# Another order at the seams of a six-stage kernel: expert stages, recurrence gates, layernorms in quarters, first rotations on another engine

## The chip, the cores and the metric

The kernel runs on one core of a Trainium2 chip. The metric is the device time of one execution in microseconds (us). A core has five engines that matter here, each of which works through its own instructions in order: PE (TensorE, the matmuls), DVE (VectorE), ACT (ScalarE), POOL (GpSimd) and SP (SyncE, which issues most of the transfers). They wait for each other through semaphores.

## The reference

The input x has 2 sequences of 2048 tokens with 256 features, 4096 tokens in all. Six residual stages follow each other:

```python
x = x + 0.5 * moe(layernorm(x))       # stage 1
x = x + attention0(layernorm(x))      # stage 2
x = x + 0.5 * moe(layernorm(x))       # stage 3, the same weights
x = x + 0.5 * rnn(layernorm(x))       # stage 4
x = x + attention1(layernorm(x))      # stage 5
x = x + 0.5 * rnn(layernorm(x))       # stage 6

# moe: sigmoid router, 2 of 6 experts, and one shared expert
w, idx = top_k(sigmoid(xt @ gate_w.T + gate_b), 2);  w = w / (sum(w) + 1e-8)
y = sum over the chosen e of w_e * ((silu(xt @ ew1[e].T) * (xt @ ew3[e].T)) @ ew2[e].T)
z = (silu(xt @ fc1.T) * (xt @ fc2.T)) @ fc3.T
moe = y + z

# attention0: 16 heads of 16 features over the full sequence of 2048, then Wff and a bias
# attention1: the same shape, causal, with rotated q and k, and relative
#             positions clipped at 32 in both the scores and the context

# rnn: the first axis (2) is the time; 2048 columns are the batch
c = in_c
for xt in x:                          # 2 steps
    f = sigmoid(xt @ wf.T + c @ uf.T + bf);  i = sigmoid(xt @ wi.T + c @ ui.T + bi)
    c = f * c + i * tanh(xt @ wc.T + c @ uc.T + bc)
rnn = tanh(x @ wo.T + c @ uo.T + bo)
```

All is computed in 32-bit floats.

## The kernel before

x stays in the on-chip memory for the whole run, as 32 chunks of 128 tokens by 256 features. Four chunks make a block (512 tokens), so there are 8 blocks; blocks 0 to 3 are the first sequence, 4 to 7 the second. The order on PE, ACT and DVE is the order in which the program issues its instructions; inside the expert stage the same holds for POOL. Nothing reorders the work afterwards, so an instruction that waits holds everything behind it on its engine. Results of matmuls go to 8 banks of 512 floats (`s` in the profile), which ACT or DVE must empty before PE can use them again.

**Layernorm** (lines 86 to 124). `stat(b, c)` runs two DVE instructions on one chunk (L95, L96), `root(b)` two on POOL for the block (L100, L102), `stats(b)` is four `stat` and the `root`. `normal(b, engine)` applies mean and scale with four instructions (L113) on DVE or POOL, `turn(b)` transposes the block on PE (L123) and copies it out on ACT (L124).

**Expert stage, `moe`** (L158 on). The router (`route`, L184) computes logits on PE (L190), copies them with ACT (L195), transposes them (L198), and picks two experts on DVE. `sort` (L237) gives each token a place per expert, `scatter(b)` (L298) writes the normalized rows of one block to those places in DRAM: 8 indirect transfers on POOL's queue. `experts(h, ...)` (L332 to L395) then works through the sorted rows of one half of the tokens, which SP loads (`xs<-places`). `combine(h, c)` (L398 to L410) fetches the two weighted results of one chunk, again with an indirect transfer on POOL (`yg`, L403), and adds them to x on DVE (L408). The shared expert is cut into `shared_up` (16 matmuls, L138, and Silu on ACT, L311), `shared_mul` (DVE, L318) and `shared_down` (16 matmuls L325, added to x by DVE, L330). An explicit list at L420 to L473 interleaves all of this: blocks 0 to 3 are normalized, routed, sorted and scattered, then 4 to 7; `experts(0)`, `experts(1)` with the chunks of the first half combined in between; at the end the shared expert of blocks 5, 6 and 7 and 16 chunks of `combine(1, c)`, 8 in a row, then block 7, then 8 more.

**Recurrence** (L730 on). `gate(cb, step, m)` makes three matmul groups for one block at one time step, activations on ACT (L781), products on DVE (L786 on). `outputs(cb)` computes both steps' outputs (L802 and L816 on PE, L821 and L827 on DVE, L824 on ACT). After `outputs(cb - 1)` a call `between(cb - 1)` runs; in the first recurrence it contains the layernorm and turn of blocks 0 and 1 for the second attention, and some preparation of its weights.

**Attentions** (L609 and L861 on). Both run through a table of steps: `jobs.at(step, fn, ...)` registers work beside the score matmuls, and the work of one step is issued in the order in which it was registered, half of it after the first and half after the second piece of the step. Score matmuls for the row maximum (L650, L969) feed DVE reductions (`mx`, L654 and L977); `subtract(t)` transposes the negative maxima of a group (L545) and adds them to q on DVE (L549), after which the scores for the exponential can be computed (L662, L1047 and L1054). `ln_stats(b, qc)` runs the statistics of one block in one step, its `normal` on POOL. In the second attention `rotate` (L890) copies a projection out of PSUM (ACT, L896), exchanges neighbours (DVE, L898) and does the multiplications and the addition on POOL (L899 to L903).

Of the kernel before, what the change touches and what calls it, by code (L numbers as in the profile page):

```python
# [17 lines left out]
P = 128  # L18
# [24 lines left out]
def macaron_kernel(ctx: ExitStack, tc: tile.TileContext, t: dict, out: bass.AP):  # L43
# [114 lines left out]
    def moe(w, ws, gate_w, gate_b, rev, tri, iota, z, behind, last):  # L158


        with ExitStack() as s:
# [9 lines left out]
            def norm(b):  # L171
                if b not in xn:
                    z.normal(b, nc.vector, keep.tile([P, CPB, D], F32, name=f"xn{b}"))
                if b not in xnT:
                    z.turn(b)

            def stats(b):
                if b not in xn:
                    z.stats(b)
# [4 lines left out]
            def route(h):  # L184
# [27 lines left out]
                col = [keep.tile([P, HC, 1], F32, name=f"col{h}{i}") for i in range(4)]  # L212
# [24 lines left out]
            def sort(h):  # L237
# [41 lines left out]
                at = place[h] = keep.tile([P, 2 * HC], mybir.dt.int32, name=f"at{h}")  # L279
# [24 lines left out]

            def shared_up(b):
                pgu = [bank() for _ in range(4)]
                for i in range(4):
                    mm2(pgu[i], ws[:, :, i // 2 * D : i // 2 * D + D], ts(i % 2, P), xnT[b])
                sgs = [wk.tile([P, TB], F32, name="sgs", bufs=4) for _ in range(2)]
                for ic in range(2):  # L310
                    nc.scalar.activation(sgs[ic], pgu[ic], AF.Silu)  # L311
                half[b] = sgs, pgu[2:]

            def shared_mul(b):
                sgs, pu = half.pop(b)
                hh[b] = wk.tile([P, 2, TB], F32, name="hh", bufs=2)
                for ic in range(2):
                    nc.vector.tensor_tensor(hh[b][:, ic, :], sgs[ic], pu[ic], ALU.mult)  # L318
# [79 lines left out]
            def combine(h, c):  # L398

                for i in range(2):  # L400
                    yg = wk.tile([P, D], F32, name="yg", bufs=6)
# [18 lines left out]
            with tc.manual_schedule(engines={mybir.EngineType.Pool}):  # L420
                for b in range(HB):
                    stats(b)
                    norm(b)
                    if b == 1:
                        up(0)
                route(0)
                mul(0)
                stats(4)
                stats(5)
                up(1)  # L430
                down(0)
                e0 = sort(0)
                scatter(0)
                stats(6)
                stats(7)
                for b in range(1, HB):
                    scatter(b)
                mul(1)
                up(2)
                norm(4)  # L440
                norm(5)
                mul(2)
                down(1)
                up(3)
                norm(6)
                norm(7)
                mul(3)
                down(2)
# [3 lines left out]
                down(3)  # L452
                e1 = sort(1)
                for b in range(HB, NTB):
                    scatter(b)
                down(4)
                experts(0, e0, lambda i: None)
                experts(1, e1, first_half)
                up(5)
                mul(5)  # L460
                up(6)
                mul(6)
                down(5)
                for c in range(8):
                    combine(1, c)
                    last(c)
                up(7)
                mul(7)
                down(6)
                down(7)  # L470
                for c in range(8, HC):
                    combine(1, c)
                    last(c)  # L473
            xnT.clear()

# [9 lines left out]
    class Pieces:  # L485
# [14 lines left out]
        def ln_stats(self, b, qc):  # L500
            blk = b * SB + qc
            self.norm.stats(blk)
            self.norm.normal(blk, nc.gpsimd)
            self.add_bias(blk)
# [104 lines left out]
    def attention0(norm, tail, wq, wk_, wv, wo, bff):  # L609
# [7 lines left out]
        with ExitStack() as s:  # L617
# [64 lines left out]
            PER = 8  # L682
            for b in range(B):
                first = b * SB * G * PER

                for qc in range(SB) if b else ():
                    at(first - 40 + 4 * qc, z.ln_stats, b, qc)
# [4 lines left out]
                for g in range(G):  # L692
                    for qc in range(SB):
                        due = first - 6 + PER * g + qc
                        at(due if b else (-1 if g == 0 else 2 * g - 1 + qc // 2), keys, b, g, qc)
# [4 lines left out]
            for t, (b, qc, g) in enumerate(groups):  # L700
                at(PER * t - 1, queries, t)
                at(PER * t + 8, z.subtract, t)
# [27 lines left out]
    def recurrence(w, norm, store, between):  # L730
# [3 lines left out]
        with ExitStack() as s:  # L734
# [106 lines left out]
            for m in range(2):  # L841
                gate(0, 0, m)
            turn(1)
            for cb in range(SB):
                if cb + 1 < SB:
                    for m in range(2):
                        gate(cb + 1, 0, m)
                if cb + 2 < SB:
                    normal(cb + 2)
                gate(cb, 1, 0)  # L850
                if cb + 2 < SB:
                    turn(cb + 2)
                gate(cb, 1, 1)
                if cb:
                    outputs(cb - 1)
                    between(cb - 1)
# [4 lines left out]
    def attention1(norm, tail, w, relk, relv, kbias, dramp, skew):  # L861
# [4 lines left out]
        with ExitStack() as s:  # L866
# [23 lines left out]
            def rotate(dst, wa, b, qc, bias):  # L890
# [8 lines left out]
                nc.gpsimd.tensor_tensor(dst, xa, cos[b, qc], ALU.mult)  # L899
                nc.gpsimd.tensor_tensor(xb, xb, sin[b, qc], ALU.mult)  # L900
                if bias is not None:
                    nc.gpsimd.tensor_scalar_add(xb, xb, bias)
                nc.gpsimd.tensor_tensor(dst, dst, xb, ALU.add)  # L903
# [240 lines left out]
            for n in range(NG):  # L1144
                at(early[n], queries, n)
            for b in range(B):
                for qc in range(SB):
# [5 lines left out]
                    if b or qc > 1:  # L1153
                        at(f - 12, z.ln_stats, b, qc)
# [6 lines left out]
            for n, (b, qc, g) in enumerate(groups):  # L1161
                at(max(By[n], early[n] + 1), by_position, n)
                at(Me[n] + 1, z.subtract, n)
# [47 lines left out]
    def run_moe(norm, behind, last, clear=False):  # L1211
        with ExitStack() as s:
# [16 lines left out]
            moe(w, ws, gate_w, gate_b, rev, tri, iota, norm, behind, last)  # L1229
# [36 lines left out]
    with tc.manual_schedule(engines=ENGINES):  # L1266

        n0, n1, n2, n3, n4, n5 = (Norm() for _ in range(6))
        with ExitStack() as s:
# [10 lines left out]
            for b in range(3):  # L1280
                tail += [(1 + 2 * b, n2.stats, b), (2 + 2 * b, n2.normal, b, nc.vector),
                         (3 + 2 * b, n2.turn, b)]
            attention0(n1, tail, *weights)
# [3 lines left out]
        with ExitStack() as s:  # L1287
# [13 lines left out]
            run_moe(n2, ahead.run, last)  # L1301
# [7 lines left out]
            def between(cb):  # L1309

                if cb == 0:
# [6 lines left out]
                if cb in (1, 2):  # L1318
                    n4.stats(cb - 1)
                    n4.normal(cb - 1, nc.vector)  # L1320
# [98 lines left out]
```

## Time and profile before

| | |
|---|---|
| median of 3 runs | 4281.56 us (4280.34 to 4281.79) |
| the profiled execution, its own time | 4388.43 us |
| its span | 4386.7 us |
| mean granted PE clock | 0.971 |
| PE busy | 4143.3 us |
| DVE, ACT, POOL busy | 2714.8, 2545.9, 1824.1 us |

The stages in this span, by the first instruction of each: first expert stage from 0, first attention from about 430, second expert stage from 2193, recurrence from 2613, second attention from 2816, second recurrence from about 4200 us.

In a row such as "PE s L123 <- DVE b L113: 16.8, 8, 8.0", PE waited before its instruction of line 123 for the DVE instruction of line 113, 16.8 us in all, 8 times, 8.0 us at most. In a timeline row the first two numbers are start and duration, and the square bracket tells how long the engine had been idle and what ended that. In a row of windows the numbers are the window, its length, the busy time of PE, of PE's weight loads, of DVE, ACT and POOL (with the number of instructions), the granted PE clock, the DMA share and the GB/s. The profiled execution is 106.9 us longer than the median of the runs.

### The profile page before, as it was taken

How to read it: one execution, taken by the hardware profiler on the slowest of the kernel's cores; microseconds unless marked ns; L12 is line 12 of the kernel's file. 1: busy time of each engine (PE TensorE's matmuls, PEld its weight loads, DVE VectorE, ACT ScalarE, POOL GpSimd, SP SyncE). 2: the span in 40 equal slices, each digit the busy share in tenths (PEclk: the TensorE clock that was granted, in tenths of full speed). 3: DMA queues.
4: the chain of work that ended last, by engine and by line, in shares of the span. 5: the costliest groups of instructions: out<-in, count | busy, mean ns of one | idle time of the engine just before them, and what ended most of it. 6: DMA issues, size and time to landing. Idle time of an engine off the chain costs nothing.

```text
span 4386.7 us, 77337 instructions
## 1 busy us (share of the span) xinstructions
PE 4143.3 (94%) x28512; PEld 1982.5 (45%) x28512; DVE 2714.8 (62%) x6176; ACT 2545.9 (58%) x5155; POOL 1824.1 (42%) x1665
## 2 busy tenths in 40 slices
PE   6798999999999999999977989799999999999999
PEld 3455433333334333333344554455554455555445
DVE  4233787877776778788551333466676666666633
ACT  2232488887877788888822313155656665566742
POOL 3226133335433333333432240375655774654510
PEclk8899999999999999999988989999999999999999
DMA  6242000000000000000043320144542234542201
GB/s 237 93 121 75 1 1 1 1 1 1 1 1 2 1 1 1 1 1 1 16 148 99 120 82 0 37 94 87 109 88 51 59 76 87 100 95 46 44 21 39
DMA packets 355514, 224.29 MB, mean 51 GB/s; under 512 B 146625, under 2 KB 338497, under 8 KB 355137
## 3 DMA queue, kind: packets, MB, share of 16 engines
q1 hardware_dynamic: 342848, 185.77, 17.2%
q0 software_dynamic: 12288, 33.57, 2.4%
q8 instruction: 227, 3.72, 0.4%
q14 instruction: 151, 1.23, 0.1%
HBM read 114.17 MB, written 105.12 MB: 50 GB/s over the span
## 4 chain that ended last, share of the span: by engine, by line
PE 85%; DVE 5%; POOL 4%; issue 3%; another core or an unknown queue 1%; ACT 1%; DMA 1%; SPq 0%; POOLq 0%; ACTq 0%; DVEq 0%
PE s L662 13%; PE s L674 11%; PE s L138 11%; PE s L650 10%; PE s L1083 6%; PE s L358 6%; PE s L969 6%; PE s L1054 5%; PE s L377 3%; PE s L592 1%; PE s L1064 1%; PE s L527 1%; PE s L1047 1%; PE s L1068 1%
## 5 line engine op out<-in xcount | busy, mean ns | idle before, releaser
L560 POOL TENSOR_TENSOR o<-o,part 128x512 f32<-128x512 f32 (+3 forms) x800 | 964.5, 1206 | 1382.1 <-ACT part L558 1378.2
L654 DVE TENSOR_REDUCE mx<-s 128x1 f32<-128x512 f32 x2048 | 1271.1, 683 | 363.7 <-PE s L650 363.4
L667 ACT ACTIVATE pT<-s 128x512 f32<-128x512 f32 x2048 | 1064.3, 617 | 205.1 <-PE s L650 203.9
L650 PE MATMUL s<-kT,q 32*128 32x512 f32 x4096 | 1014.5, 618 | 7.3 <-DVE mx L654 6.0
L662 PE MATMUL s<-q,kT 32*128 32x512 f32 x4096 | 1014.9, 615 | 6.3 <-DVE q L549 5.4
L1075 ACT ACTIVATE pT<-s 128x512 f32<-128x512 f32 (+3 forms) x1280 | 589.0, 541 | 243.4 <-PE s L1054 105.7
L662 PEld LDWEIGHTS s<-q,kT 32*128 32x128 f32 x4096 | 414.5, 184 | 471.4 <-DVE mx L654 310.5
L558 ACT COPY part<-s 128x512 f32<-128x512 f32 (+3 forms) x800 | 466.1, 584 | 240.2 <-PE s L1083 118.5
L977 DVE TENSOR_REDUCE mx<-s 128x1 f32<-128x512 f32 (+1 forms) x768 | 472.8, 678 | 188.7 <-PE s L969 180.1
L674 PE MATMUL s<-pT,v 128*32 128x512 f32 x4096 | 549.9, 605 | 2.0 <-DVE mx L654 1.9
L650 PEld LDWEIGHTS s<-kT,q 32*128 32x128 f32 x4096 | 405.1, 184 | 138.5 <-ACT pT L667 71.6
L969 PE MATMUL s<-kT,q 32*128 32x512 f32 (+7 forms) x2240 | 333.3, 436 | 4.9 <-ACT part L558 4.6
L358 PE MATMUL s<-we,xT 128*128 x592 | 289.9, 613 | 35.3 <-issue 25.8
L1083 PE MATMUL s<-pT,v 128*32 128x512 f32 (+3 forms) x2560 | 305.5, 545 | 2.3 <-DVE mx L977 1.2
L365 DVE TENSOR_TENSOR h<-sg,s 128x256 f32<-128x256 f32 x148 | 62.1, 421 | 350.0 <-ACT sg L363 299.9
L403 POOL DMA_INDIRECT yg<-results,at x128 | 125.9, 984 | 310.6 <-PE s L358 104.3
L969 PE MATMUL s<-b,q 32*128 32x512 f32 (+7 forms) x1280 | 238.9, 517 | 7.4 <-POOL b L903 4.0
L993 DVE CUSTOM_DVE_ANT_0 band<-s,band 128x160 f32<-128x160 f32 (+1 forms) x512 | 155.7, 316 | 142.4 <-PE s L969 78.3
L1054 PE MATMUL s<-q,kT 32*128 32x512 f32 (+3 forms) x1152 | 240.5, 516 | 0.0
L674 PEld LDWEIGHTS s<-pT,v 128*32 128x32 f32 x4096 | 82.1, 108 | 337.6 <-ACT pT L667 281.9
L1054 PE MATMUL s<-q,b 32*128 32x512 f32 (+3 forms) x896 | 210.7, 568 | 0.0
L1007 POOL TENSOR_TENSOR band<-band,mneg 128x640 f32<-128x640 f32 x128 | 161.3, 1262 | 100.1 <-DVE mneg L1003 99.8
(208 smaller groups left out, 5554.8 us busy)
## 6 DMA issues: line engine op xcount, KB each, us to landing
band<-skew SPq DMA_DIRECT2D x32, 1280.0 KB
pd<-band SPq DMA_DIRECT2D x32, 1280.0 KB
xs<-places SPq DMA_DIRECT2D x148, 128.0 KB
results<-y SPq DMA_DIRECT2D x148, 128.0 KB
places<-zero SPq DMA_DIRECT2D x2, 4736.0 KB
we<-in_we SPq DMA_DIRECT2D x12, 768.0 KB
skew<-s SPq DMA_DIRECT2D x32, 256.0 KB
s<-pd SPq DMA_DIRECT2D x32, 256.0 KB
```

Of the source, the lines that this page charges most:

```text
L138: nc.tensor.matmul(ps, lhsT=w[:, kc, cols], rhs=rhs[:, kc, :], start=start and kc == 0, stop=stop and kc == 1,)
L358: nc.tensor.matmul(pu, lhsT=xT[i][:, ts(kc, P)], rhs=w[:, kc, ds(val[i], 2 * D)], start=kc == 0, stop=kc == 1,)
L560: nc.gpsimd.tensor_tensor(o, o, part[:, q0:], ALU.add)
L650: nc.tensor.matmul(ps, lhsT=q[t][rows(j), ts(qb, P)], rhs=kT[b, g][rows(j), ts(kc, TB)], start=True, stop=True,)
L654: nc.vector.tensor_reduce(mx[t][:, qb * J + j, kc : kc + 1], ps, AX.X, ALU.max)
L662: nc.tensor.matmul(st, lhsT=kT[b, g][rows(j), ts(kb, P)], rhs=q[t][rows(j), :], start=True, stop=True,)
L667: nc.scalar.activation(z.pTs[t, kb, j], st, AF.Exp)
L674: nc.tensor.matmul(pv[rows(j), :], lhsT=v[b, g // 2][:, kb, ds(h * VW, 32)], rhs=z.pTs.pop((t, kb, j)), start=True, stop=True,)
L969: nc.tensor.matmul(ps[:, ds(cols, n)], lhsT=lhsT, rhs=kT[b, c, g][rows(j), ds(k0, n)], start=True, stop=True,)
L1054: nc.tensor.matmul(ps[:, q0:], lhsT=k, rhs=q[t][rows(j), q0:], start=True, stop=True, skip_group_check=True,)
L1075: nc.scalar.activation(z.pTs[t, kb, j][:, q0:], st.pop((t, kb, j))[:, q0:], AF.Exp)
L1083: nc.tensor.matmul(pv[rows(j), q0:], lhsT=v[b, kb // CPB, g // 2][:, kb % CPB, ds(h * VW, 32)], rhs=z.pTs.pop((t, kb, j))[:, q0:], start=T ...
```

## The change

1. The explicit order of the expert stage is rewritten. Statistics of several blocks are issued ahead of the normalizations, the first shared block is computed in four parts between them, `sort(0)` follows the router with only one block's `up` in between, the scatters of blocks 0 to 3 are spread out, and the shared expert's `up`, `mul` and `down` of block 5 come ahead of `experts(0)`. Each Silu directly follows its matmuls (`shared_part`), with 6 buffers instead of 4.
2. At the end, the chunks of `combine(1, c)` are issued in portions (2, 1, 1, 4, then all others) between the shared expert's pieces of blocks 6 and 7. In the second expert stage the last 8 chunks are not issued there but by the recurrence, two after each of its first four gates (`rest`), with 12 buffers for the fetched rows instead of 6.
3. In the first recurrence the layernorms for the second attention are issued ahead of a gate of the second step and their turns behind it (`normals`, `turns`).
4. In both attentions the layernorm statistics are issued one chunk a step, `subtract` is registered ahead of all other work of its step, and in the first attention eight instead of four key projections precede the first step.
5. Rotations of steps before 0 do their multiplications and additions on DVE instead of POOL.

```diff
 def norm(b):
+    normal(b)
+    if b not in xnT:
+        z.turn(b)
+def stats(b):
+    if b not in xn and b not in z.mv:
+        z.stats(b)
+def normal(b):
     if b not in xn:
         z.normal(b, nc.vector, keep.tile([P, CPB, D], F32, name=f"xn{b}"))
...
+def shared_part(b, i):
+    ps = bank()
+    mm2(ps, ws[:, :, i // 2 * D : i // 2 * D + D], ts(i % 2, P), xnT[b])
+    if i < 2:
+        sgs = wk.tile([P, TB], F32, name="sgs", bufs=6)
+        nc.scalar.activation(sgs, ps, AF.Silu)
+        ps = sgs
+    half.setdefault(b, []).append(ps)
...
-                    yg = wk.tile([P, D], F32, name="yg", bufs=6)
+                    yg = (wk if gathered is None else gathered).tile(
+                        [P, D], F32, name="yg", bufs=6 if gathered is None else 12
+                    )
...
-for b in range(HB):
-    stats(b)
-    norm(b)
-    if b == 1:
-        up(0)
-route(0)
+stats(0); stats(1); norm(0); stats(2); norm(1)
+shared_part(0, 0); shared_part(0, 1)
+stats(3); norm(2)
+shared_part(0, 2); norm(3); shared_part(0, 3)
 mul(0)
 stats(4)
+route(0)
+up(1)
+e0 = sort(0)
 stats(5)
-up(1)
 down(0)
-e0 = sort(0)
 scatter(0)
-stats(6)
-stats(7)
-for b in range(1, HB):
-    scatter(b)
 mul(1)
 up(2)
+stats(6); up(3); scatter(1); mul(2)
 norm(4)
 norm(5)
-mul(2)
+stats(7); scatter(2); scatter(3)
 down(1)
-up(3)
+mul(3); down(2)
 norm(6)
 norm(7)
-mul(3)
-down(2)
+down(3)
 route(1)
 up(4)
 mul(4)
-down(3)
 e1 = sort(1)
+down(4); up(5); mul(5)
 for b in range(HB, NTB):
     scatter(b)
-down(4)
+down(5)
 experts(0, e0, lambda i: None)
 experts(1, e1, first_half)
-up(5)
-mul(5)
 up(6)
 mul(6)
-down(5)
-for c in range(8):
-    combine(1, c)
-    last(c)
+rest(2)                  # two chunks of combine(1, c) and last(c)
 up(7)
 mul(7)
+rest(1)
 down(6)
+rest(1)
 down(7)
-for c in range(8, HC):
-    combine(1, c)
-    last(c)
+rest(4)
+if gathered is None:
+    rest(HC)
...
-        def ln_stats(self, b, qc):
+        def ln_stats(self, b, qc, c):
             blk = b * SB + qc
-            self.norm.stats(blk)
-            self.norm.normal(blk, nc.gpsimd)
-            self.add_bias(blk)
+            self.norm.stat(blk, c)
+            if c == CPB - 1:
+                self.norm.root(blk)
+                self.norm.normal(blk, nc.gpsimd)
+                self.add_bias(blk)
...
+            for t in range(NG):
+                at(PER * t + 8, z.subtract, t)
...
-                    at(first - 40 + 4 * qc, z.ln_stats, b, qc)
+                    for c in range(CPB):
+                        at(first - 43 + 4 * qc + c, z.ln_stats, b, qc, c)
...
-                        at(due if b else (-1 if g == 0 else 2 * g - 1 + qc // 2), keys, b, g, qc)
+                        at(due if b else (-1 if g < 2 else 2 * g - 1 + qc // 2), keys, b, g, qc)
...
             for m in range(2):
                 gate(0, 0, m)
+                rest(2)
             turn(1)
             for cb in range(SB):
                 if cb + 1 < SB:
                     for m in range(2):
                         gate(cb + 1, 0, m)
+                        rest(2)
                 if cb + 2 < SB:
                     normal(cb + 2)
+                normals(cb)
                 gate(cb, 1, 0)
                 if cb + 2 < SB:
                     turn(cb + 2)
+                turns(cb)
                 gate(cb, 1, 1)
                 if cb:
                     outputs(cb - 1)
-                    between(cb - 1)
...
-                nc.gpsimd.tensor_tensor(dst, xa, cos[b, qc], ALU.mult)
-                nc.gpsimd.tensor_tensor(xb, xb, sin[b, qc], ALU.mult)
+                e = nc.vector if step < 0 else nc.gpsimd
+                e.tensor_tensor(dst, xa, cos[b, qc], ALU.mult)
+                e.tensor_tensor(xb, xb, sin[b, qc], ALU.mult)
                 if bias is not None:
-                    nc.gpsimd.tensor_scalar_add(xb, xb, bias)
-                nc.gpsimd.tensor_tensor(dst, dst, xb, ALU.add)
+                    e.tensor_scalar_add(xb, xb, bias)
+                e.tensor_tensor(dst, dst, xb, ALU.add)
...
             for n in range(NG):
+                at(Me[n] + 1, z.subtract, n)
+            for n in range(NG):
                 at(early[n], queries, n)
...
-                        at(f - 12, z.ln_stats, b, qc)
+                        for c in range(CPB):
+                            at(f - 13 + c, z.ln_stats, b, qc, c)
                         at(f - 7, z.ln_transpose, b, qc)
...
-            def between(cb):
-                if cb == 0:
-                    ...
-                if cb in (1, 2):
-                    n4.stats(cb - 1)
-                    n4.normal(cb - 1, nc.vector)
-                    n4.turn(cb - 1)
-                    n4.xn.pop(cb - 1)
+            def normals(cb):
+                if cb == 1:
+                    ...                      # the same preparation of a["q"], relk, relv
+                if cb > 1:
+                    n4.stats(cb - 2)
+                    n4.normal(cb - 2, nc.vector)
+            def turns(cb):
+                if cb > 1:
+                    n4.turn(cb - 2)
+                    n4.xn.pop(cb - 2)
```

## Prediction

> **What bounds the kernel now.** I read the page's busy shares and chain first, then the table of windows, then the waits of PE, and last the timeline around the longest of these waits.
>
> ```profile
> span 4386.7 us, 77337 instructions
> PE 4143.3 (94%) x28512; PEld 1982.5 (45%) x28512; DVE 2714.8 (62%) x6176; ACT 2545.9 (58%) x5155; POOL 1824.1 (42%) x1665
> PEclk8899999999999999999988989999999999999999
> PE 85%; DVE 5%; POOL 4%; issue 3%; another core or an unknown queue 1%; ACT 1%; DMA 1%; SPq 0%; POOLq 0%; ACTq 0%; DVEq 0%
> ```
>
> PE bounds the span. The change takes no matmul away, so it can only win PE's idle time, 4386.7 - 4143.3 = 243 us, and what PE loses at a low clock. The clock row dips in two places, the two expert stages.
>
> ```profile
> 410.00:433.00 23.00, 16.84 (x52) 9.57 (x52) 10.77 (x21) 3.35 (x5) 14.51 (x16) 0.78 0.30 86
> 2590.00:2633.00 43.00, 24.39 (x83) 15.71 (x84) 18.85 (x47) 4.37 (x7) 23.57 (x25) 0.72 0.26 74
> 2816.00:2870.00 54.00, 41.05 (x213) 21.22 (x213) 34.29 (x103) 9.63 (x16) 48.65 (x39) 0.87 0.35 83
> 2870.00:4200.00 1330.00, 1292.01 (x11338) 673.83 (x11337) 859.07 (x2562) 837.91 (x1778) 790.21 (x697) 0.99 0.37 78
> ```
>
> [...] The seams are poor (24.4 of 43 us busy at clock 0.72), attention is full. POOL is busy 48.65 of 54 us at the second attention's start.
>
> ```profile
> PE s L198 <- ACT lgT L195: 38.4, 4, 18.9
> PE s L123 <- DVE xn L113: 29.1, 4, 8.9
> PE s L325 <- DVE hh L318: 19.0, 2, 17.8
> PE s L123 <- DVE b L113: 16.8, 8, 8.0
> 98.89 0.59 ACT L195 COPY lgT<-s 128x512 f32<-128x512 f32 x1 [20.68 <-remote]
> 405.37 3.62 PE L325 MATMUL s<-ws,hh 128*128 128x256 f32 x16
> 415.47 6.65 PE L325 MATMUL s<-ws,hh 128*128 128x256 f32 x16 [6.49 <-DVE x L408]
> 423.95 1.07 POOL L403 DMA_INDIRECT yg<-results,at  x1 [3.97 <-DVE x L408]
> 2758.27 0.45 PE L123 MATMUL s<-ident,b 128*128 128x128 f32 x1 [7.13 <-DVE b L113]
> 1016.81 0.66 PE L662 MATMUL s<-q,kT 32*128 32x512 f32 x1 [1.41 <-DVE q L549]
> 2831.32 1.18 PE L969 MATMUL s<-b,q 32*128 32x480 f32 x4 [4.02 <-POOL b L903]
> ```
>
> The longest wait is a doubtful one. The lgT copy needs only a matmul that ended at 80.6, yet runs at 98.9, when the last of 24 scatters in a row has been issued; PE, ACT and DVE all crawl until then. Four such stretches (19 and 20 us in the first expert stage, 18 and 21 in the second), with their half-clock restarts, come to some 100 us. The profiled execution took 4388.4 us, the median of the runs is 4281.6: 107 us less. I therefore take the crawl to belong to the profiled execution, win nothing there, and set the sum of the other stalls against 4281.6.
>
> **The change part by part.**
>
> *Second expert stage into recurrence.* The shared expert's up is 16 matmuls, 7.0 us; its down 3.6 us. Ahead of the gap at 2589.05 PE does up(5), up(6), up(7), down(5), down(6) = 28.3 us, so the experts end at about 2560.7 (the same count gives 381 in the first stage). The first gate matmul comes at 2617.4, 56.7 us later: DVE has 16 gathered rows and two layernorms in front of hh of block 7 (the 17.8 us wait). Afterwards PE has up(6), up(7), down(6), down(7) = 21.2, the bias matmuls L746 2.7, the turn 1.7: 25.6 us. That is 31 us less, 10.6 of which are up(5) and down(5), now in front. The 1.3 us wait for gf goes too. Is DVE in time? The 16 gathers ahead of the recurrence start 3.4 us after the experts (384.7 against 381.3), at a pitch of 1.255 us, and land 2.7 us later: DVE reaches the first bias at +27 us, ACT needs it at about +31. The other 16 gathers (20 us on POOL), 16 adds (0.48 us each) are cut into fours behind the first four gates (12 matmuls, 5.2 us each); four gathers take 5.0 us, so the cover is thin, but they start 3 us ahead. Were the cover gone, they would cost 5 us for each of four. Twelve buffers instead of six let POOL run ahead. **32 us.**
>
> *Front, both stages.* With scatters 0 to 3 out earlier (sort(0)'s 6.3 us DVE chain no longer queues behind two blocks of statistics, 2 x 2.1 us, and a 1.25 us add), the 8.7 us wait at 50.6 goes, with about 3 us of half clock; up(5) and down(5), 10.6 us, come in ahead of experts(0). New: the roots of blocks 6 and 7 stand on POOL behind 8 and 16 scatters of 1.27 us, so norm(7) may hold DVE and PE about 3 us; the 32 scatters of blocks 4 to 7 pass no other work on POOL. SP's loads of xs wait for scatters 0 to 3 as before. The experts start about 2 us later with 10.6 us more done: **-2 us each**, between +5 and -8; the first stage's scatter might also be held by the 4.7 MB fill of places, whose landing I can't see.
>
> *First expert stage into attention.* Here the end is set by POOL: 32 gathers took from 384.7 to 436.35, 51.6 us, though 32 x 1.255 = 40.2; in the rest POOL waited for buffers while DVE stood at mul and down (3.97 us in the row above, 7.9 at 392). With two chunks, mul(7), then single chunks between the downs, the buffers come free in time: 11 us. The clock (6.65 against 3.62 us for the same 16 matmuls): 1.5. Four more keys (7 us of PE) drawn into the wait of 5.95 us at 433.4: 3, since the half-steps they leave fall to what DVE allows, 2.5 instead of 3.0 us. **15 us.**
>
> *Recurrence.* The turns wait 7.13 and 7.96 us for a layernorm behind outputs on DVE (2.1 statistics, 1.5 root, 1.4 normal). They move to a gate of 24 matmuls, 10.6 us. The first is covered; for the second DVE's output tail runs 7 us past PE, and 7 + 5 - 10.6 leaves 1.5. So 13.5. The four a_q/relk operations move under another gate, where they cost nothing; without cover they are 4 x 0.7 = 3 us. The half clock after each gap is a window of 6.8 us, 4.5 us of it busy: 2 us each. **17 us.**
>
> *First rotations on VectorE.* POOL ran 11 operations of 1.27 to 1.57 us from 2816.8 to 2831.3. DVE's tensor_tensor of this shape takes 0.69 (L786); with three shuffles of 0.73 the same takes 9.8 us: b at 2826.7, 4.6 us earlier. Half clock: 1.5. Behind them on DVE's queue stand the first mx reductions, which can't start before b. **6 us**, from 0 to 11. Here a rule speaks against the change. The row: POOL 1.27 us an operation while DVE idles 7.6 us. The Trainium skill, "SBUF — State Buffer", section "SBUF: two separate sides", says that a VectorE operation with two SBUF inputs and a GpSimd operation that reads SBUF exclude each other for the whole instruction. If each of the 11 met a 1.27 us POOL operation, that would be 14 us and the part would lose 8. But the change empties POOL there (its zeroing of v ends at 2815.6), so I keep 6; the row of later rotations decides.
>
> *Layernorm in quarters, subtract first.* In the first attention PE waited 0.93 + 1.41 us twice, because four pairs of statistics (2.1 us) stood ahead of subtract; one pair (0.53) behind it now. 4.7 + 1.5 half clock = 6. In the second: 4.06 us at 2859, half of 5.6 us near 3380 to 3396 (POOL's normal of 4 x 1.22 us stays), and half clock 3: 9. The last quarter comes two steps later, three steps ahead of its turn; a step is about 8.7 us (statistics 2860.5, turn 2903.8, five steps), POOL needs 6.1. **15 us.**
>
> The clock is the second place where row and rule part:
>
> ```profile
> 1069.60:1073.00 3.40, 1.42 (x12) 0.27 (x10) 3.37 (x8) 1.64 (x4) 2.46 (x3) 1.00 0.00 0
> 1073.00:1076.40 3.40, 3.03 (x16) 1.32 (x16) 1.14 (x3) 0.96 (x2) 3.40 (x4) 0.56 0.00 0
> ```
>
> In these 3.4 us PE still worked 1.42 us, and the next 3.4 us ran at 0.56. "TensorE: Matmul & The Clock Gate", Part 1, lets the half clock follow a whole idle window of about 3.4 us; by that, waits of 1 to 3 us cost only themselves, and this part would be worth about 3 us less. The measurement decides, but not each time: the twin waits at 1013.4 and 1015.4 were followed by clock 1.00. So I count one half-clock window here, not two, and my rows of clock stand (about 17 us of the sum in all).
>
> Tiles moved to smaller buffers and the Silu right after its matmul: nothing, ACT is 58% busy and idle there.
>
> Sum: 32 - 4 + 15 + 17 + 6 + 15 = 81 us, 4281.6 - 81 = 4200.
>
> **The rivals.**
>
> (1) *Stalls move.* DVE and POOL run in order. rest(2) makes DVE wait for gathers inside the recurrence, the roots wait behind scatters, mx behind the rotations. For: DVE's waits for yg were 31.8 us in 38. Price: 4 x 5 us in the recurrence, 2 x 8 in front, 6 at the rotations = 42: 4242. Against: POOL is only 10.31 us busy in the recurrence.
>
> (2) *The crawl is real in all runs.* It begins some 11 scatters into a row. The first row, 24 long, is cut to 8, 8, 16: 14 us less in each stage, 28 in all: 4172. Against: the 107 us.
>
> (3) *Slower: subtract waits at PE's head.* Subtract's four transposes are registered first in each of 64 groups; PE is in order, and they need the last mx of the group. If each waited for DVE's last four reductions (2.45 us), that is 157 us, and 4281.6 - 81 + 157 = 4358. It decides from 1.3 us a group (81 / 64). Against: PE's waits for L545 before are 0.4 us in all, and only steps with another job change.
>
> (4) *The diff does less than it says*: the starts stay bound by ws, fill and gathers, the gaps re-form elsewhere: within 0.2%.
>
> **How the numbers follow.** Main case 60%: 4175 to 4225. Rival 1, 22%: 4225 to 4262. Rival 2, 11%: 4150 to 4180. Rival 3, 3%. Rival 4, 4%. 0.2% is 8.6 us, about what a measurement of this kernel can tell from no change. The range 4163 to 4245 leaves out the slow half of rival 1, part of rival 2, and rivals 3 and 4: under 20%. Faster 0.93, same 0.04, slower 0.03.
>
> **What would show it.** Right: L325 <- hh from 19 to under 4 us; L123 <- b under 5; the last yg of the first stage some 44 us after the experts; PE busy over 90% between the experts' end and the second attention; no 8.7 us gap before L123 near 50. The profiled span should fall by about as much as the runs, and more only if the scatters' crawl shrinks. Wrong: waits of PE for L781 or DVE's x L408 inside the recurrence (rival 1), long waits before L545 (rival 3), POOL's rotations slowed by DVE.

## The result and the profile after

The changed kernel takes 4205.97 us (median of 4 runs, 4205.13 to 4206.97), the kernel before 4281.37 us beside it (4280.34 to 4281.79). That is 75.4 us less, a ratio of 0.9824 (95% interval 0.9807 to 0.9841). On two of the chips used, every run of the kernel before takes about 4393 us instead of 4281, and its trace shows all engines late beside the scatters (the crawl, below); the profile shown of before comes from such an execution, those of after from one without it, so the spans of the two must not be subtracted.

The page of the kernel after: span, busy time, granted clock and the chain that ended last.

```profile
span 4204.5 us, 77295 instructions
PE 4101.3 (98%) x28512; PEld 1966.6 (47%) x28512; DVE 2720.4 (65%) x6190; ACT 2542.8 (60%) x5155; POOL 1804.3 (43%) x1651
PEclk9999999999999999999999999999999999999999
PE 90%; DVE 4%; POOL 3%; issue 1%; DMA 1%; ACT 1%; SPq 0%; POOLq 0%; ACTq 0%; DVEq 0%
```

PE is now busy for 98% of the span and both dips of the clock row are gone. What is left shows in the waits of PE (total, times, longest):

```profile
PE s L123 <- DVE xn L113: 25.8, 6, 9.4
PE s L123 <- DVE b L113: 15.5, 7, 12.0
PE s L682 <- DVE mx L686: 8.9, 1, 8.9
PE s L1007 <- DVE b L941: 3.3, 1, 3.3
PE s L202 <- ACT lgT L199: 3.0, 4, 0.8
PE s L335 <- DVE hh L328: 0.4, 2, 0.2
```

(L123 is the layernorm's turn, L202, L335 and L682 are the old L198, L325 and L650, L1007 is the old L969.) The 17.8 us wait for hh fell to 0.4 in all, and the 8.7 us gap near 50 is gone. But the turns did not fall below 5 us as foretold: they wait 12.0 us in the recurrence, behind its first two gates, and 6.4 us in each front (the stretch of an expert stage ahead of its first expert matmul). The windows around the seams, in the columns used before:

```profile
345.00:384.00 39.00, 29.46 (x97) 15.90 (x96) 19.34 (x39) 6.69 (x10) 27.98 (x52) 0.94 0.33 97
2446.00:2497.00 51.00, 38.15 (x130) 22.09 (x130) 19.87 (x51) 6.60 (x11) 30.10 (x32) 0.89 0.36 112
2672.00:2697.00 25.00, 21.06 (x125) 10.67 (x124) 23.55 (x74) 2.93 (x5) 15.60 (x13) 0.93 0.50 126
2697.00:4002.00 1305.00, 1285.86 (x11371) 670.07 (x11372) 870.26 (x2591) 838.21 (x1780) 801.83 (x708) 0.99 0.36 79
```

The two new waits before L123 in the timeline, with what stands ahead of them on POOL and DVE:

```profile
72.10 0.96 POOL L303 DMA_INDIRECT places<-xn,at  x1 [0.30 <-issue]
73.09 0.24 POOL L100 TENSOR_SCALAR ve<-mv 128x4 f32<-128x4 f32 x1
75.06 1.03 PE L123 MATMUL s<-ident,xn 128*128 128x128 f32 x3 [6.42 <-DVE xn L113]
...
2490.11 0.25 POOL L100 TENSOR_SCALAR ve<-mv 128x4 f32<-128x4 f32 x1
2491.59 1.06 POOL L102 TENSOR_TENSOR rstd<-ve,mhalf 128x4 f32<-128x4 f32 x1
2492.68 1.42 DVE L113 TENSOR_SCALAR b<-x,mv,rstd 128x256 f32<-128x256 f32 x4 [9.42 <-POOL rstd L102]
2493.24 1.03 PE L123 MATMUL s<-ident,b 128*128 128x128 f32 x3 [12.00 <-DVE b L113]
```

Both are a root (0.24 + 1.04 us of work) that waits on POOL behind indirect transfers: 8 scatters at 73, and at 2490 a row of 17 gathers, of which the last 9 are for chunks that nobody needs yet. DVE had the statistics ready at 2483.2, so about 8 of the 12.0 us are the root's (6.9 us until it starts, 1.2 for a gather between its two instructions).

For the accounting every trace is divided at the starts of the same instructions: the first expert matmul (L368), the last one (L387), the 65th score matmul of the first attention (L682) and its last (L694), the first and last expert matmul of the second stage, the first gate matmul, the first rotated product (L970), the 41st score matmul behind it that reads a kT and the last score matmul (L1092). Lengths in us; the last recurrence with the way to it is 204 to 205 us in all of them. The rotation of the first q lies ahead of its product, so it counts in the column recurrence.

| kernel | crawl | front 1 | experts 1 | tail 1 | attention 1st | front 2 | experts 2 | tail 2 | recurrence | start | attention 2nd |
|---|---|---|---|---|---|---|---|---|---|---|---|
| before | yes | 117.5 | 263.6 | 81.6 | 1723.7 | 111.6 | 263.2 | 56.2 | 205.7 | 25.0 | 1333.6 |
| before_again | yes | 118.3 | 265.8 | 80.8 | 1724.2 | 111.0 | 264.5 | 54.5 | 208.4 | 25.1 | 1333.8 |
| after | no | 107.7 | 227.6 | 67.9 | 1715.5 | 101.3 | 225.8 | 25.0 | 198.6 | 22.8 | 1307.3 |
| after_again | no | 107.6 | 227.6 | 67.9 | 1715.6 | 101.3 | 225.8 | 25.0 | 198.6 | 22.8 | 1304.4 |
| old_front | no | 100.4 | 227.6 | 79.3 | 1715.4 | 90.9 | 227.5 | 35.3 | 198.5 | 22.8 | 1304.5 |
| old_ln | no | 109.4 | 227.6 | 68.1 | 1724.8 | 99.6 | 225.8 | 25.0 | 198.4 | 22.8 | 1331.6 |
| pool_order | no | 110.0 | 227.6 | 68.2 | 1715.5 | 99.3 | 225.8 | 25.0 | 198.2 | 22.8 | 1308.8 |
| no_rest | yes | 115.2 | 261.7 | 71.3 | 1715.5 | 109.2 | 256.9 | 25.0 | 209.8 | 23.9 | 1307.9 |
| old_turns | yes | 116.0 | 260.9 | 70.4 | 1715.5 | 107.6 | 266.9 | 25.0 | 218.5 | 22.1 | 1305.5 |
| pool_rot | yes | 115.7 | 262.3 | 71.0 | 1715.5 | 108.5 | 264.9 | 25.0 | 201.6 | 26.0 | 1304.1 |
| late_subtract | yes | 118.1 | 257.7 | 70.9 | 1718.0 | 109.2 | 265.9 | 25.5 | 197.2 | 22.8 | 1307.2 |
| pool_wrap | yes | 118.4 | 257.7 | 71.0 | 1715.6 | 108.5 | 266.6 | 25.5 | 194.9 | 22.6 | 1307.7 |
| roots_first | yes | 127.5 | 259.9 | 70.4 | 1715.6 | 118.4 | 266.2 | 25.0 | 198.9 | 22.7 | 1307.9 |
| best | yes | 127.2 | 261.6 | 58.6 | 1718.8 | 118.4 | 266.4 | 25.0 | 196.3 | 22.8 | 1307.6 |

Among the kernels with the order of after, only the fronts and the experts differ with the crawl, and tail 1 by some 3 us; the first attention and the stages from tail 2 on agree across chips. Traces with the same order in a stage differ by up to 3 us in the recurrence, by almost 5 in the second attention and, with the crawl, by 10 in the experts; a smaller difference in one trace of these stages says little. On the crawling chips the changed kernel itself was not run, and on the other before was not profiled; there each kernel is read by its stage against the others.

### The profile page after: what moved, and what is told of

It reads as the page before. It is cut to its first block, busy times and chain, and to the rows that moved or that the text cites. A ratio compares the mean times of both kernels' runs of the same rounds, so it can differ in the third digit from the quotient of the medians.

```text
span 4204.5 us, 77295 instructions
## 1 busy us (share of the span) xinstructions
PE 4101.3 (98%) x28512; PEld 1966.6 (47%) x28512; DVE 2720.4 (65%) x6190; ACT 2542.8 (60%) x5155; POOL 1804.3 (43%) x1651
## 4 chain that ended last, share of the span: by engine, by line
PE 90%; DVE 4%; POOL 3%; issue 1%; DMA 1%; ACT 1%; SPq 0%; POOLq 0%; ACTq 0%; DVEq 0%
PE s L694 13%; PE s L138 12%; PE s L706 12%; PE s L682 10%; PE s L1121 6%; PE s L368 6%; PE s L1007 6%; PE s L1092 6%; PE s L387 3%; PE s L624 1%; PE s L559 1%; PE s L1102 1%; PE s L1106 1%; PE s L1085 1%; PE s L850 1%
## 5 line engine op out<-in xcount | busy, mean ns | idle before, releaser
L699 ACT ACTIVATE pT<-s 128x512 f32<-128x512 f32 x2048 | 1063.5, 617 | 196.3 <-PE s L682 195.4
L682 PE MATMUL s<-kT,q 32*128 32x512 f32 x4096 | 1015.2, 620 | 10.2 <-DVE mx L686 8.9
L694 PE MATMUL s<-q,kT 32*128 32x512 f32 x4096 | 1011.3, 614 | 0.0
L694 PEld LDWEIGHTS s<-q,kT 32*128 32x128 f32 x4096 | 414.1, 183 | 462.9 <-DVE mx L686 307.7
L682 PEld LDWEIGHTS s<-kT,q 32*128 32x128 f32 x4096 | 410.7, 184 | 139.4 <-ACT pT L699 73.1
L1007 PE MATMUL s<-kT,q 32*128 32x512 f32 (+7 forms) x2240 | 329.1, 433 | 0.3 <-DVE mx L1036 0.3
L368 PE MATMUL s<-we,xT 128*128 x592 | 278.9, 593 | 1.1 <-ACT xT L363 1.1
L1007 PE MATMUL s<-b,q 32*128 32x512 f32 (+7 forms) x1280 | 234.8, 509 | 3.5 <-DVE b L941 3.3
L1092 PE MATMUL s<-q,kT 32*128 32x512 f32 (+3 forms) x1152 | 237.4, 508 | 0.0
L1092 PE MATMUL s<-q,b 32*128 32x512 f32 (+3 forms) x896 | 211.0, 569 | 0.1
```

Of the source, the lines that this page charges most:

```text
L368: nc.tensor.matmul(pu, lhsT=xT[i][:, ts(kc, P)], rhs=w[:, kc, ds(val[i], 2 * D)], start=kc == 0, stop=kc == 1,)
L682: nc.tensor.matmul(ps, lhsT=q[t][rows(j), ts(qb, P)], rhs=kT[b, g][rows(j), ts(kc, TB)], start=True, stop=True,)
L694: nc.tensor.matmul(st, lhsT=kT[b, g][rows(j), ts(kb, P)], rhs=q[t][rows(j), :], start=True, stop=True,)
L699: nc.scalar.activation(z.pTs[t, kb, j], st, AF.Exp)
L1007: nc.tensor.matmul(ps[:, ds(cols, n)], lhsT=lhsT, rhs=kT[b, c, g][rows(j), ds(k0, n)], start=True, stop=True,)
L1092: nc.tensor.matmul(ps[:, q0:], lhsT=k, rhs=q[t][rows(j), q0:], start=True, stop=True, skip_group_check=True,)
```

## The experiments

On a first chip, with the crawl (before: 4393.4 us):

**before_again**: no edit.

> The kernel before, unchanged, profiled once more. Theory 1 (the crawl beside long rows of scatters belongs to that one profiled execution): the span comes out near 4281 us, PE's wait for lgT falls from 38.4 us to under 5, the mean clock rises to about 0.985. Theory 2 (the profiler brings the crawl to this kernel each time): the span is again near 4387 us with the clock near 0.971.

Measured: 4393.0 us, clock 0.972, and seven more runs of before on that chip took 4391.1 to 4397.6. Theory 1 falls with this. Theory 2, which these runs fit, falls with the second chip: seven runs of before there, whose span and clock were read in the same way, took 4280.1 to 4283.2. So neither one execution nor the profiler makes the crawl; it goes with the chip, or with the time at which a chip was used, since no chip was used at two different times. The variants of the changed kernel showed it too on the chips that crawl. The same stretch, from the end of the front into the experts, first no_rest with the crawl, then after_again without:

```profile
104.00:150.00 46.00, 24.05 (x66) 11.66 (x64) 9.10 (x24) 3.73 (x9) 30.66 (x32) 0.80 0.30 103
```

```profile
104.00:150.00 46.00, 45.76 (x182) 28.24 (x181) 11.62 (x29) 14.41 (x42) 26.88 (x29) 1.00 0.49 163
```

POOL issues scatters in both. On one chip PE does 66 matmuls beside them, on the other 182, and is busy for 45.76 of the 46 us.

**no_rest**: the second stage issues all its chunks itself.

```diff
-rest = run_moe(n2, ahead.run, last, gathered=pool(s, "gathered"))
+rest = run_moe(n2, ahead.run, last)
```

> The kernel after, but the second expert stage issues all its combine chunks itself (6 buffers), none in the recurrence. Main theory (hidden adds are what the tail won): DVE and POOL work off 16 more gathers (20 us) ahead of the first gate's activations, of which the changed kernel already waits 12 us; so 8 to 20 us slower than the changed kernel, 4214 to 4226. Rival (the order in front of block 7's mul won it all, the place of the last chunks is worth nothing): within 4 us of 4206.

Measured: 4303.0 us; its recurrence 209.8 us against 198.6, so 11.2 us slower in that stage, as the main theory had it. Its waits of PE name the place:

```profile
PE s L123 <- DVE x L420: 20.9, 1, 20.9
```

**old_turns**: the second attention's layernorm goes back behind the outputs.

```diff
-                normals(cb)
                 gate(cb, 1, 0)
...
-                turns(cb)
                 gate(cb, 1, 1)
                 if cb:
                     outputs(cb - 1)
+                    normals(cb)
+                    turns(cb)
```

> The kernel after, with the layernorm and turn of the second attention's first two blocks back behind outputs(cb - 1). Main theory: the waits of 7.1 and 8.0 us before L123 and their half clock come back, 15 to 19 us slower than 4206: 4221 to 4225. Rival (part of it was only moved: the changed kernel waits 2 us at a turn and DVE is later elsewhere): 8 to 13 us slower.

Measured: 4316.6 us; its recurrence takes 218.5 us against 198.6, 19.9 us more, at the upper end of the main theory. Waits of PE in this kernel:

```profile
PE s L123 <- DVE b L113: 30.6, 9, 12.0
```

That is 15.1 us more than the 15.5 of the kernel after, and its timeline has the waits of before in them (7.13 and 7.95 us). The other 4.8 us are busy time: in the recurrence PE takes 187.6 us for the matmuls that took 182.7, at a granted clock of 0.93 instead of 0.96.

**pool_rot**: `e = nc.gpsimd` for all rotations.

> The kernel after, with the first rotations back on POOL. Main theory: the waits of 4.1 and 4.0 us at the start of the second attention come back in place of 0.7 and 3.3: 4 to 7 us slower than 4206. Rival (VectorE and GpSimd hinder each other, or the rotations now delay the first reductions, so that nothing was won): within 2 us of 4206.

Measured: 4300.3 us. The start of the second attention takes 26.0 us against 22.8, and the recurrence, which ends with the first q rotation, 201.6 against 198.6: 6.2 us, as the main theory had it. Both waits are back, in pool_rot:

```profile
2764.38 2.08 PE L970 MATMUL s<-relk,q 128*128 128x128 f32 x8 [4.09 <-POOL q L941]
2772.65 1.98 PE L1007 MATMUL s<-b,q 32*128 32x480 f32 x8 [3.77 <-POOL b L941]
```

In the kernel after:

```profile
2667.26 0.67 DVE L937 TENSOR_TENSOR q<-s,cos 128x512 f32<-128x512 f32 x1
2669.41 1.13 PE L970 MATMUL s<-relk,q 128*128 128x128 f32 x8 [0.69 <-DVE q L941]
2674.70 0.69 DVE L941 TENSOR_TENSOR b<-b,s 128x512 f32<-128x512 f32 x1
2675.54 1.09 PE L1007 MATMUL s<-b,q 32*128 32x480 f32 x8 [3.28 <-DVE b L941]
```

The waits are 3.9 us shorter in all, and the 16 matmuls behind them take 2.2 us instead of 4.1. DVE does not slow down: from its first shuffle to the end of b it needs 8.8 us, where POOL needs 14.4 from its first operation. The second wait stays because DVE's operations, too, come one after another.

On a second chip, without the crawl (before: 4282.1 us):

**after_again**: no edit.

> The changed kernel, unchanged, so that the kernels of this call have their own reference. Theory 1 (beside long rows of scatters all engines crawl in some sessions and not in others, whatever the kernel): either 4206 us beside 4281 for before, or some 4296 beside 4393. Theory 2 (the change removed the crawl): 4206 in any session.

Measured: 4204.1 us (4202.2 to 4206.5). By itself this fits both theories; the variants on the first chip, which share its fronts and still crawl, exclude Theory 2.

**old_ln**: four statistics in one step and subtract in its old place.

```diff
-for t in range(NG):
-    at(PER * t + 8, z.subtract, t)
...
-for c in range(CPB):
-    at(first - 43 + 4 * qc + c, z.ln_stats, b, qc, c)
+at(first - 40 + 4 * qc, z.ln_stats, b, qc, 0)
...
 at(PER * t - 1, queries, t)
+at(PER * t + 8, z.subtract, t)
...
-for n in range(NG):
-    at(Me[n] + 1, z.subtract, n)
...
-for c in range(CPB):
-    at(f - 13 + c, z.ln_stats, b, qc, c)
+at(f - 12, z.ln_stats, b, qc, 0)
...
 at(max(By[n], early[n] + 1), by_position, n)
+at(Me[n] + 1, z.subtract, n)
```

> The changed kernel with the statistics of a block in one step again and subtract registered where it was. Main theory: the waits of 0.9 + 1.4 us (twice), 4.1 us and 5.6 us and their half clock come back, 10 to 16 us slower than after_again. Rival (what DVE does not do there it does later, PE's waits for POOL's o stay): under 6 us slower.

Measured: 4238.5 us, 34.4 slower than after_again. Both theories asked for less than half of that. 9.2 us fall in the first attention, 27.2 in the second. The second attention of old_ln, its window and its waits of PE:

```profile
2706.00:4036.00 1330.00, 1296.53 (x11373) 673.80 (x11372) 870.34 (x2592) 838.78 (x1780) 802.13 (x709) 0.99 0.35 77
```

```profile
PE s L600 <- POOL o L591: 8.2, 3, 3.5
PE s L1082 <- DVE q L580: 7.9, 4, 3.8
PE s L1004 <- ACT part L589: 6.8, 3, 3.1
```

In the kernel after, the same part of the trace has

```profile
PE s L601 <- POOL o L592: 3.2, 1, 3.2
PE s L577 <- DVE mneg L1041: 3.0, 3, 1.3
```

and no wait for part among the larger ones. Against the window 2697 to 4002 of the kernel after, PE is idle 33.5 instead of 19.1 us, and takes 10.7 us more for as many matmuls. So 14 us are waits and 11 us slower matmuls. The trace records 30.7 us at half clock in this window and 17.1 in that of after, which accounts for about 7 of the 11; the other 4 stay open.

**old_front**: the list of before up to `experts(0)`, with `up(5); mul(5)` and `down(5)` behind the experts. Two things of the change stay in it: each Silu directly behind its matmuls, and an edit that the list of the change leaves out, the statistics of block 3 of the second expert stage at the end of the first attention.

> The changed kernel with the order of before up to experts(0) in both expert stages, and block 5 of the shared expert behind the experts again. Main theory (the front is worth 4 us over both stages, and the tail pays 2 x 10.6 us of PE, hidden beside gathers in the first stage only): 8 to 16 us slower than after_again. Rival (the front's order won much more than the 4 us that the prediction gave it, because experts(0) no longer waits): 25 to 40 us slower.

Measured: 4208.4 us, 4.3 slower: under what both theories asked. The old front is 7.2 and 10.4 us shorter, the tails 11.4 and 10.3 us longer. Its experts wait for their first rows:

```profile
PE s L361 <- DMA xs<-places: 4.7, 2, 2.4
```

In tail 1 the last 16 chunks are still issued in portions, but with block 5 back behind the experts their 32 gathers take 51.0 us again (331.3 to 382.3), as before (50.7), and not the 40 of the kernel after.

**pool_order**: POOL held to the order of the program (`manual_schedule`) in the recurrence too.

> The changed kernel with POOL kept in the order of the program in the first recurrence too, so that the root of block 5 runs before the last 16 gathers. Main theory (the 12.0 us wait before L123 is the root standing behind gathers that were put ahead of it): the wait falls to about 4 us, with some half clock 8 to 11 us faster than after_again. Rival (the layernorm is late because the chunks before it are): within 3 us.

Measured: 4206.2 us (4202.0 to 4207.1), the same as after_again. It decides nothing: POOL's order came out as it was, 17 gathers between the roots of blocks 4 and 5, because the root is issued by the expert stage and the gathers by the recurrence, in two separate regions.

On a third chip, again with the crawl (before: 4392.5 us):

**late_subtract**: the two subtract edits of old_ln alone.

> The changed kernel with subtract registered in its old place, the statistics still one chunk a step. In old_ln both were undone, for 34 us, 19 more than the prediction gave the part. Theory 1 (the place of subtract within its step won most): 20 us or more slower than the changed kernel, whose time was 4204 to 4206 beside 4281 to 4282 for before. Theory 2 (the bursts of statistics cost nearly all of it, ahead of mx, exp and POOL's o as well as ahead of subtract): under 8 us slower.

Measured: 4300.0 us. The first attention takes 1718.0 us against 1715.5, the second 1307.2, as after. This is Theory 2 for the place of subtract: 2.5 us, once the statistics are spread. The rest of old_ln's loss needs the bursts of statistics; the bursts with subtract first were not run, so how much of it an early subtract would save beside them is open.

**pool_wrap**: one region around both.

```diff
+with tc.manual_schedule(engines={mybir.EngineType.Pool}):
     rest = run_moe(n2, ahead.run, last, gathered=pool(s, "gathered"))
...
     recurrence(rec, n3, False, rest, normals, turns)
```

> The changed kernel with POOL held to the order of the program across the second expert stage's end and the recurrence; the root of block 5 now runs before the last 16 gathers, where it ran behind 9 of them (pool_order had left POOL's order as it was). Theory 1 (the 12.0 us wait before L123 is that root): the wait falls to about 4 us, 8 to 11 us faster than the changed kernel. Theory 2 (the chunks before it are late, or the gathers now hold the gates): within 3 us.

Measured: 4297.5 us. Between the experts and the second attention the waits of PE before L123 were, in the kernel after and then in pool_wrap,

```profile
PE s L123 <- DVE b L113: 14.4, 3, 12.0
```

```profile
PE s L123 <- DVE b L113: 7.7, 4, 3.3
```

The 12.0 us wait is 3.0 us, so 9 us of it were the root behind gathers. But the gathers come later now, and two waits of 1.1 and 3.35 us come before the next turns. Tail 2 and recurrence take 220.4 us against 223.6: 3.2 us won of the 8 to 11 expected. The win is small but there: best, which has the same edit, takes 221.3, the kernels without it (and with the rotations of after) 222.7 to 223.9. PE's idle time falls by 6.8 us there, but the same matmuls take 3.6 us longer.

**roots_first**: `stats(7)` ahead of `scatter(1)`.

> The changed kernel with the statistics and root of block 7 ahead of the scatter of block 1. Theory 1 (the 6.4 us wait before L123 in each expert stage is that root standing behind 8 scatters): the wait goes; 2 x 6.4 and some half clock, less what experts(0) then waits for xs: 10 to 16 us faster. Theory 2 (experts(0) starts when the scatters of blocks 0 to 3 have landed, whatever PE does before): within 4 us.

Measured: 4317.3 us, slower than late_subtract and pool_wrap on the same chip by 17 to 20. The 6.4 us wait is gone, and this takes its place in the waits of PE:

```profile
PE s L202 <- ACT lgT L199: 42.0, 4, 20.4
```

This is the wait of before, in both stages. Without the root between them, 24 scatters stand in a row again. Where the crawl is, the root of block 7, of all things, kept the row short: the fronts take 127.5 and 118.4 us with the long row, 118.1 and 109.2 (late_subtract, the same chip) with the short ones. What this edit does without the crawl was not run.

**best**: pool_wrap, roots_first, and the first stage's last chunks in the first attention.

```diff
+for t in range(8):
+    at(2 + 2 * t, rest, 1)
```

> pool_wrap and roots_first together, and the last 8 combine chunks of the first expert stage issued by the first attention, one every second step from step 2. Theory 1 (the 8.8 us wait before L682 is mx standing behind combines that nothing needs yet): 9 us and some half clock on top of the two others, 25 to 38 us faster than the changed kernel. Theory 2 (adds and gathers among the attention's reductions cost DVE what they win): only the sum of the two others.

Measured: 4305.1 us, not the best. It has roots_first's long row. But tail 1 takes 58.6 us against 71.0 (pool_wrap), the first attention 1718.8 against 1715.6: the chunks moved into the attention win 12.4 - 3.2 = 9.2 us, about what Theory 1 gave them. Together with pool_wrap and without roots_first that should be some 12 us, worked out from these stages and not run.

## Why the prediction was right, and where it was not

4200 was foretold, 4206 came; the main case held its range. That it came so close is in part luck: one term was 19 us too small, three were 13, 14 and 4 us too large, and they made up for each other. Right in mechanism and size were the second tail, the turns and the rotations.

| part | predicted | measured | from |
|---|---|---|---|
| second expert stage to the first gate | 31 | 31.2 | tail 2, before to after (29.5 from before_again) |
| the same, first bias and turns in time | 1 | -12 | the new wait before L123 |
| fronts | -4 | -17.6 | after against old_front, 7.2 + 10.4 |
| first expert stage into attention | 15 | 10.7 | tail 1 with the crawl: before 81.6, late_subtract 70.9 |
| turns in the recurrence | 17 | 19.9 | old_turns |
| first rotations | 6 | 6.2 | pool_rot, recurrence and start |
| statistics and subtract | 15 | 34.4 | old_ln |
| sum | 81 | 73 | runs: 75.4 and, on the second chip, 78.0 |

- **The second tail, right.** The count of matmuls ahead of the first gate, 25.6 us, came out as 25.0, and the part of block 5, 10.6, as 10.3 (old_front, 35.3).
- **"With two chunks, mul(7), then single chunks between the downs, the buffers come free in time: 11 us", in the first tail.** The gathers did end 10 us earlier after the experts (44 to 45 us behind them, as foretold), but not by the portions alone: in old_front, which has them, tail 1 takes 79.3 us and the gathers 51. The 11.4 us came with block 5, whose leaving I had booked at nothing in this tail because POOL sets its end. And the tail still ends with 8.86 us of waiting for mx behind adds; best showed 9.2 us there. The Silu's place and the four more keys were not run alone.
- **"DVE reaches the first bias at +27 us."** It came at about +48. I counted gathers and adds in front of the first bias, and not the two layernorms that `last` issues at chunks 3 and 7, nor that POOL's order is free from the recurrence on. pool_wrap shows that the root's place made 9 of the 12 us. The -12 of the table is the length of the wait; undoing its cause won 3.2 us of time.
- **"The experts start about 2 us later", in the fronts.** They started 7.2 and 10.4 us later. sort(0) did become earlier (at by 45.6 instead of 51.5), but the first scatter went out at 51.33 instead of 51.81, since the root of block 5 stands ahead of it. And the wait for the root of block 7, which I put at 3 us, is 6.4, with 1.2 for block 6 and a half clock behind it. The whole front still pays 4.3 us, because up(5) and down(5) leave the tails, which are 11.4 and 10.3 us shorter.
- **"Half of 5.6 us" and "POOL's normal stays", in the second attention.** The term was 9 of 27.2 us (its own parts add to 9.9). I took only waits whose named releaser was subtract or mx, and left aside those for POOL's o and ACT's part as untouched. They go with the burst, too: late_subtract, with the statistics spread, has no wait for part and 4.7 us for o, old_ln 6.8 and 8.2. That the burst reaches them by way of DVE being late, then ACT, then POOL is argued from the order of the work, not traced. And the matmuls behind the waits were slower, 11 us in all. The place of subtract, which I named as the cause, is worth 2.5 us where the statistics are spread.
- **The clock.** The rows were the better guide, also for short waits. In old_ln PE worked 1.58 of 3.4 us, with no wait longer than 1.82, and the next 3.4 us ran at half clock (0.50), which costs 1.7 us:

```profile
3385.50:3388.90 3.40, 1.58 (x13) 0.65 (x12) 1.51 (x9) 1.56 (x4) 3.40 (x6) 1.00 0.66 211
3388.90:3392.30 3.40, 3.40 (x20) 1.70 (x22) 0.80 (x4) 1.58 (x4) 3.40 (x4) 0.50 0.00 0
```

- **Rotations, right.** The durations were as foretold (0.67 to 0.69 us), and b ended 5.7 us sooner. The exclusion of VectorE and GpSimd by the Trainium skill ("SBUF — State Buffer", section "SBUF: two separate sides") had no object here, as POOL was idle from 2665.4 to 2680.9, past the last of these operations; no run here puts the two beside each other.
- **"I take the crawl to belong to the profiled execution."** Wrong in its cause: on two chips every run has it. It didn't touch the forecast, because the runs behind the given median (4280.3 to 4281.8) do not have it. Rival 2's mechanism is real where the crawl is: with the row of 24 scatters the fronts of roots_first are 9 us longer each, though its 6.4 us waits are gone.
- **Rival 3** did not come: PE waited for L577, subtract's transposes, 5.6 us in all (3.0, 2.3 and 0.3 us by releaser), not 157.
- **Rival 1** came in part: the roots behind scatters as it said, in the recurrence a root behind gathers, and not the adds between the gates.

What stops the engines in a crawl is open: the traces show PE, ACT and DVE late behind semaphores whose releasers had long ended, and end it with the last scatter, but not by what.

## What to carry to other kernels

Before a small instruction's place is called free, look at what shares its in-order queue: a root of 1.3 us behind a row of transfers, issued one every 1.25 to 1.27 us, made two new waits here (6.4 and 12.0 us). When a burst on one engine delays another, count every wait downstream of it for the next microseconds, whatever releaser the row names, and the half clock after them. When work is moved from one place to another, ask of both places what sets their length: here the block that left the first tail won more than the new order inside it. Take a profile and its times from one chip, or check a stage that shouldn't differ, before subtracting one from the other.

## What the runs showed of the hardware that I had not expected

The same program took 4280 to 4283 us on one chip and 4390 to 4398 us on two others. Whether that is the chip or the time at which it was used is not separated, since none was used at two different times. Between kernels with the order of after, nearly all of the difference lies in the fronts and the experts (experts 226 to 228 against 257 to 267 us), in which GpSimd issues rows of indirect scatters; tail 1 differs by 3 us, and the other stages by no more than traces of one chip. The rows of gathers, in the tails, brought nothing like it. The row's length matters: PE waited 20 us for lgT with 24 scatters in a row (roots_first), 2 to 3 us with 8, 8 and 16 (its neighbours with the crawl).
